# A neighbour search kept as marks, and softplus as one ScalarE function, in a graph-convolution and state-space kernel

## The chip, the cores and the metric

The kernel runs on one core of a Trainium2 chip. The metric is the time of one execution on the device in microseconds (us). Before the change the median of three runs is 13028.27 us (13025.54 to 13030.78). The engines are called PE (TensorE), DVE (VectorE), ACT (ScalarE), POOL (GpSimd) and SP (SyncE, which only issues DMAs here). Each works off its own queue of instructions.

## The reference

Two layers follow each other on x of shape (16, 96, 64, 64), all in fp32. Layer 0 is a graph convolution over windows of 8 x 8 pixels; for each of the 64 pixels of a window it finds the 9 nearest of the 64 by cosine distance, and takes the maximum over them:

```python
y = affine(conv1x1(x, fc1_w, fc1_b), fc1_s, fc1_t)
nodes = window_partition(y, 8).reshape(Bw, C, 64).transpose(0, 2, 1)
_, idx = jax.lax.top_k(-dist(nodes / norm), 9)
x_j = vmap(lambda n, i: n[i])(nodes, idx)
feat = concatenate([x_i, x_j - x_i], -1)            # x_i: the pixel itself
h = gelu((einsum('bnkc,oc->bnko', feat, ew) + eb) * es + et)
y = max(h, over the 9 neighbours)
x = affine(conv1x1(y, fc2_w, fc2_b), fc2_s, fc2_t) + x
```

Layer 1 has two Mamba blocks over the 4096 pixels in sequence (192 inner channels, 16 states), then a fusion with the pooled input, a batch normalisation and a residual:

```python
xc = silu(causal_conv4(h @ in_w)[..., :192]);  z = second half of h @ in_w
dt, Bm, Cm = split(xc @ xproj_w)
delta = softplus(dt @ dt_w + dt_b)
h_t = exp(delta * A) * h_(t-1) + delta * Bm * xc     # 16 states, 192 channels
y = (sum over the states of h_t * Cm + Dp * xc) * silu(z)
seq = seq + y @ out_w
```

## The kernel before

**Work and rows.** Layer 1 is cut into 256 items: 16 images, 2 blocks, 8 tiles of 512 pixels. The 192 channels and 16 states of an item are worked off in 8 rows, p = 0 to 7, of two states each, so that a row is a tile of 128 partitions by 3 x 512. There are 2048 rows, and the main loop (L871) makes one in each turn. A row is

- bt (`bcast`, L729): PE spreads B of the two states over the partitions, in the one PSUM buffer of its pool; it is issued at the head of the turn before,
- db (`times_b`, L734): DVE multiplies u = delta * xc by bt, at the end of the turn before, after that turn's scan,
- da (`chosen`, L708): ACT computes exp(delta * A), three instructions of 128 x 511, up to two rows ahead, into one of four buffers,
- hb (L911): DVE runs the recurrence as a scan over 1536 columns,
- hb times C (L943): POOL,
- y (`folded`, L745 and L747): PE adds the two states of each channel into PSUM, one turn later, at the end of the turn.

**Steps in the background.** All other work is written as generators, advanced by one step a turn between the scan and the fold: `prelude` of the next item but one (started in row 4, L888: projections pj with silu, xproj pd, softplus, delta and u), `norm`, `tail` (pow, the output product), `carry` (the state handed from tile to tile), and layer 0: `nearest` and `edges` of one image tile per 16 rows (the tiles 4 to 8 go faster, as do the first ones, ahead of the loop). So a cycle of 16 rows holds two items and one layer-0 tile, whose two halves (four windows each) have their gelu block in rows 2 and 3 and in rows 10 and 11. The order of each engine's queue is the order in which this program writes the instructions (`manual_schedule`, L807). A step that yields TABLE (gelu, silu) holds back the da of that turn, so that ACT changes its function table seldom; `preload_act_table_set` after the gelu block (L503) and after silu (L627) brings back the table of exp and ln.

**PSUM.** All background products share one pool, `pm` (L205), with two buffers under one tag, mm: a product can start once the product two before it in the program has been read out, mostly by ACT.

**Neighbours.** `nearest` computes the scores of a tile (sc, scs), then on DVE the 8 largest of each row (L396) and their positions (L397, `max_index`); the pixel itself is masked out of the scores beforehand and added later. The positions go to DRAM (L401) and come back to 64 partitions (L430, idb). `edges` makes one-hot matrices of them: for one pair of windows on POOL by a comparison (L441), for the other on ACT by |x - node| and relu(1 - x) (L443, L444). PE multiplies them with the transformed nodes (L468, L471); gelu follows (L476), and DVE takes the maximum over the neighbours (L413).

**Softplus.** In `prelude`, one step after pd and its copy dbl, in rows 0 and 8 of a cycle: the two dt products (L646 and L649, 128 x 512 and 128 x 256), from which ACT takes Abs and Relu out of PSUM (L653, L654), then Exp, + 1, Ln and - 1 over several rows (L656 to L662); POOL adds up (L672, L674, L676) so that small arguments keep their accuracy. Eight DMAs spread the result to delta over the partitions, POOL makes delta * xc (L681), and eight more spread it to u.

Of the kernel before, what the change touches and what calls it, by code (L numbers as in the profile page):

```python
# [21 lines left out]
def tile_conv_knn_mamba(ctx: ExitStack, tc: tile.TileContext, w: dict, out: bass.AP):  # L22
# [8 lines left out]
    nc = tc.nc  # L31
# [4 lines left out]
    NN = WS * WS  # L36
    K = 9
    KO = K - 1
# [28 lines left out]
    node = const.tile([NN, 1], F32, name="node")  # L67
    nc.gpsimd.iota(node, pattern=[[0, 1]], base=0, channel_multiplier=1, allow_small_or_imprecise_dtypes=True)
    minus_node = const.tile([NN, 1], F32, name="minus_node")
    nc.vector.tensor_scalar(minus_node, node, -1.0, None, ALU.mult)  # L70
# [237 lines left out]
    def half(h):  # L308
        return slice(h * CB, (h + 1) * CB)
# [21 lines left out]
    def nearest(b, q):  # L331
# [61 lines left out]
        idx = pr.tile([128, NP, KO], U16, tag="idx", name=f"idx_{nm}")  # L393
        for p in range(NP):
            m1 = pr.tile([128, KO], F32, tag="m1", name=f"m1_{nm}_{p}")
            nc.vector.max(m1, scs[:, p, :])  # L396
            opening.append(partial(nc.vector.max_index, idx[:, p, :], m1, scs[:, p, :]))  # L397
            yield SLOT

        idx_d = dram.tile([NP, 128, KO], U16, tag="idx_d", name=f"idxd_{nm}")  # L400
        nc.sync.dma_start(out=idx_d.rearrange("p i k -> i p k"), in_=idx)  # L401
        chosen_of[b, q] = idx_d
# [13 lines left out]
    def edges(b, q):  # L416
# [3 lines left out]
        idx_d = chosen_of.pop((b, q))  # L420
# [7 lines left out]
        for hf in range(2):  # L428
            idb = pr.tile([NN, NP, NN * KO], U16, tag="idb", name=f"idb_{nm}_{hf}", bufs=1)
            nc.sync.dma_start(  # L430
                out=idb.rearrange("j w n -> j (w n)"),
                in_=idx_d.rearrange("(s p) i k -> s (p i k)", s=2)[hf : hf + 1].to_broadcast([NN, NP * NN * KO]),
            )
            yield


            for p in (1, 0):
                ohj = ohs[p][0:NN].rearrange("j w i k -> j w (i k)")
                numbers = idb[:, 2 * p : 2 * p + 2, :]
                if p == 0:  # L440
                    nc.gpsimd.tensor_scalar(ohj, numbers, node, None, ALU.is_equal)  # L441
                else:
                    nc.scalar.activation(ohj, numbers, AF.Abs, bias=minus_node)  # L443
                    nc.scalar.activation(ohj, ohj, AF.Relu, bias=1.0, scale=-1.0)  # L444
                yield
# [147 lines left out]
    def prelude(n):  # L593
# [47 lines left out]


        e = pr.tile([128, Q + QH], F32, tag="e", name=f"e_{nm}", bufs=1)
        rl = pr.tile([128, Q + QH], F32, tag="rl", name=f"rl_{nm}", bufs=1)
        va = pm.tile([128, Q], F32, tag="mm", name=f"pdta_{nm}")
        nc.tensor.matmul(va, lhsT=dt_w[i][:, :128], rhs=dbl, start=True, stop=True)  # L646
        vb = pm.tile([128, QH], F32, tag="mm", name=f"pdtb_{nm}")
        for h in range(2):
            nc.tensor.matmul(  # L649
                vb[half(h)], lhsT=dt_w[i][:, 128:], rhs=dbl[:, bass.ts(h, QH)], start=True, stop=True  # L650
            )
# [5 lines left out]
        s1 = pr.tile([128, Q + QH], F32, tag="s1", name=f"s1_{nm}", bufs=1)  # L657
        nc.scalar.activation(s1, e, AF.Identity, bias=1.0)
        yield
        ln = pr.tile([128, Q + QH], F32, tag="ln", name=f"ln_{nm}", bufs=1)  # L660
        nc.scalar.activation(ln, s1, AF.Ln)
        nc.scalar.activation(s1, s1, AF.Identity, bias=neg1)  # L662
# [14 lines left out]
        yield  # L677
        delta = pr.tile([128, NB3, Q], F32, tag="delta", name=f"delta_{nm}")
# [192 lines left out]
    for m, (n, p) in enumerate(order):  # L871
# [17 lines left out]
        if p == 5 and k + 1 < NQ:  # L889
            going.append(carry(n + 1))  # L890
# [33 lines left out]
        if p == 0:  # L924
            step_on(preps)
# [88 lines left out]
```

## Time and profile before

The profiled execution took 13021.43 us, 7 us under the median of the runs; its span is 13019.7 us.

| engine | busy us | share of the span | largest groups, us |
|---|---|---|---|
| DVE | 11940.4 | 92% | scan L911 6863.5; db L734 3605.3; maximum L413 890.4 |
| POOL | 11686.0 | 90% | hb times C L943 7091.9; one-hot L441 731.0 |
| PE | 11254.7 | 86% | y L745 2273.8 and L747 1259.5; t L468 1012.8; pj L608 932.8 |
| ACT | 10407.8 | 80% | da L708 3937.7; gelu L476 1181.3; table loads 1050 of 1.283 us |

The mean granted clock of PE is 0.949. The first scan starts at 263 us and the last at 12814 us. Between, a cycle of 16 rows takes 97 us once the slow pace of layer 0 is reached.

How to read it: a group's line gives the line of the code, the engine, the operation, what it writes and reads, how many there are, their busy time and the mean of one, and then the idle time of the engine ahead of them with what ended it. A line of waits says who waited for whom, the total in us, how often and the longest. A line of the timeline gives start and length in us; "x4" are four merged instructions. A table of stages has, after the stage's length, the busy time of PE, of PE's weight loads, of DVE, ACT and POOL (with numbers of instructions), then PE's granted clock, the DMA share and GB/s. The names y and t, pf and so on are the tiles of the program without their numbers. The matmuls in fp32 stand in the trace as two instructions each.

### The profile page before, as it was taken

The numbers are of one execution on the slowest core, as the hardware profiler recorded it, in microseconds if no ns is written. First come the engines' busy times: TensorE is split into PE (matmuls) and PEld (weight loads), VectorE is DVE, ScalarE is ACT, GpSimd is POOL, SyncE is SP. The second block draws the span as 40 slices with busy tenths as digits, with TensorE's granted clock in tenths as the row PEclk, the third lists the DMA queues.
The fourth block names the chain that finished last, engine by engine and source line by source line (L and its number), as shares of the span: only waits on it lengthen the run. The fifth ranks groups of instructions, "written<-read, shape, count | busy, mean of one in ns | idle before, by whom it ended". The sixth has DMA issues, their size and how long they took to land.

```text
span 13019.7 us, 155850 instructions
## 1 busy us (share of the span) xinstructions
PE 11254.7 (86%) x46920; PEld 4359.3 (33%) x46920; DVE 11940.4 (92%) x8270; ACT 10407.8 (80%) x16186; POOL 11686.0 (90%) x8644
## 2 busy tenths in 40 slices
PE   5889889888989989888888888988888888889872
PEld 2333333333333333333333333333333333333320
DVE  2699999999999999999999999999999999999995
ACT  4778888888888888888888888888888888888763
POOL 3699999999999999999999999999999999999993
PEclk8899999999999999999999999999999999999986
DMA  1233333333333333333333333333333333333336
GB/s 38 66 85 95 91 91 93 94 92 89 98 89 90 96 92 90 93 94 89 95 95 87 98 92 90 94 92 93 90 95 92 90 95 93 92 89 97 89 87 261
DMA packets 1031198, 1226.82 MB, mean 94 GB/s; under 512 B 429440, under 2 KB 560910, under 8 KB 1024208
## 3 DMA queue, kind: packets, MB, share of 16 engines
q1 hardware_dynamic: 1026352, 1191.59, 35.2%
q10 hardware_dynamic: 4000, 25.28, 0.5%
q8 instruction: 370, 6.06, 0.2%
q14 instruction: 476, 3.90, 0.1%
HBM read 706.83 MB, written 85.72 MB: 61 GB/s over the span
## 4 chain that ended last, share of the span: by engine, by line
POOL 27%; PE 19%; DVE 18%; ACT 13%; issue 9%; DMA 7%; SPq 6%; POOLq 0%; DVEq 0%; ACTq 0%
POOL hb L943 16%; DVE hb L911 11%; DVE db L734 6%; ACT da L708 5%; PE y L745 3%; SPq L690 2%; SPq L692 2%; DMA ct<-cd 2%; POOL ln L674 2%; PE t L468 2%; PE y L747 1%; PE pj L608 1%; PE t L471 1%; POOL hn L591 1%; POOL ln L676 1%
## 5 line engine op out<-in xcount | busy, mean ns | idle before, releaser
L943 POOL TENSOR_TENSOR hb<-hb,ct 128x1536 f32<-128x1536 f32 x2048 | 7091.9, 3463 | 313.5 <-DVE hb L911 78.4
L911 DVE TENSOR_TENSOR_SCAN hb<-da,db 128x1536 f32<-128x1536 f32 x2048 | 6863.5, 3351 | 216.6 <-ACT da L708 39.4
L708 ACT ACTIVATE da<-delta,a 128x511 f32<-128x511 f32 x6144 | 3937.7, 713 | 28.7 <-DVE hb L911 24.1
L734 DVE TENSOR_TENSOR db<-u,bt 128x1536 f32<-128x1536 f32 x2048 | 3605.3, 1760 | 386.6 <-PE bt L729 266.3
L745 PE MATMUL y<-hb,fold 128*64 128x512 f32 x8192 | 2273.8, 634 | 230.4 <-POOL hb L943 219.7
L476 ACT ACTIVATE da<-t,eb,es 128x512 f32<-128x512 f32 x1536 | 1181.3, 777 | 775.3 <-PE t L468 534.7
L747 PE MATMUL y<-hb,fold 128*64 128x256 f32 x8192 | 1259.5, 386 | 0.0
L729 PE MATMUL bt<-bparts,bsel 128*128 128x512 bf16 x2048 | 828.4, 404 | 462.4 <-DVE db L734 459.3
L468 PE MATMUL t<-oh,vu 128*128 128x512 f32 x2048 | 1012.8, 616 | 27.2 <-ACT da L476 14.1
L747 PEld LDWEIGHTS y<-hb,fold 128*64 128x64 f32 x8192 | 604.2, 141 | 1247.6 <-issue 1247.6
L413 DVE TENSOR_REDUCE hq<-da 128x192 f32<-128x1536 f32 x512 | 890.4, 1739 | 105.4 <-ACT da L476 105.4
L608 PE MATMUL pj<-hn,conv_in 128*128 128x512 f32 x2048 | 932.8, 598 | 0.9 <-POOL hn L591 0.9
L745 PEld LDWEIGHTS y<-hb,fold 128*64 128x64 f32 x8192 | 495.0, 141 | 1278.5 <-issue 528.6
L441 POOL TENSOR_SCALAR oh<-idb,node 64x1024 f32<-64x1024 uint16 x256 | 731.0, 2855 | 117.2 <-DMA idb<-idxd 111.6
L452 PE MATMUL pv<-ewT,y 96*64 96x192 f32 x2048 | 477.6, 360 | 335.2 <-ACT rs L588 253.4
L942 POOL COPY state<-hb 128x3 f32<-128x3 f32 x1792 | 397.5, 222 | 392.3 <-DVE hb L911 359.0
L620 ACT ACTIVATE xc<-pj,conv_b 128x512 f32<-128x512 f32 (+1 forms) x512 | 297.2, 580 | 510.5 <-PE pj L613 397.8
L471 PE MATMUL t<-oh,vu 128*64 128x512 f32 x2048 | 560.4, 626 | 167.0 <-ACT da L476 162.3
L608 PEld LDWEIGHTS pj<-hn,conv_in 128*128 128x128 f32 x2048 | 396.4, 194 | 386.5 <-issue 375.7
L613 PE MATMUL pj<-hn,conv_in 128*64 128x256 f32 x4096 | 514.4, 394 | 0.0
L452 PEld LDWEIGHTS pv<-ewT,y 96*64 96x64 f32 x2048 | 253.0, 143 | 774.4 <-ACT rs L588 358.4
L468 PEld LDWEIGHTS t<-oh,vu 128*128 128x128 f32 x2048 | 373.5, 194 | 402.9 <-issue 290.3
(180 smaller groups left out, 17972.0 us busy)
## 6 DMA issues: line engine op xcount, KB each, us to landing
ct<-cd SPq DMA_DIRECT2D x4096, 128.0 KB
delta<-ln SPq DMA_DIRECT2D x1024, 128.0 KB
u<-s SPq DMA_DIRECT2D x1024, 128.0 KB
idb<-idxd SPq DMA_DIRECT2D x256, 256.0 KB
delta<-ln SPq DMA_DIRECT2D x1024, 64.0 KB
u<-s SPq DMA_DIRECT2D x1024, 64.0 KB
x<-in_x SPq DMA_DIRECT2D x128, 192.0 KB
rn<-r4d SPq DMA_DIRECT2D x128, 192.0 KB
```

The lines of the kernel that those rows point to most:

```text
L413: nc.vector.tensor_reduce(out(), g.rearrange("p s (i k) -> p s i k", k=KO), AX.X, ALU.max)
L441: nc.gpsimd.tensor_scalar(ohj, numbers, node, None, ALU.is_equal)
L468: nc.tensor.matmul(t, lhsT=vus[p][:, part, :128], rhs=ohw[part], start=True, stop=True)
L476: nc.scalar.activation(g, t, AF.Gelu, bias=e_b[:, j : j + 1], scale=e_s[:, j : j + 1])
L608: nc.tensor.matmul(ps, lhsT=wt[:, t, :128], rhs=hn[:, off : off + Q], start=(t == 0), stop=(t == taps - 1))
L708: nc.scalar.activation(da[:, c, 1:Q], delta[:, c, 1:], AF.Exp, scale=a_neg[i][:, c, p : p + 1])
L729: nc.tensor.matmul(bt, lhsT=bsel[:, p, :], rhs=made[n][2], start=True, stop=True)
L734: nc.vector.tensor_tensor(db, made[n][5], bt.unsqueeze(1).to_broadcast([128, NB3, Q]), ALU.mult)
L745: nc.tensor.matmul(y[half(h), 0], lhsT=fold, rhs=hb[:, h, :], start=False, stop=(p == NPR - 1))
L747: nc.tensor.matmul(y[half(h), 1, :QH], lhsT=fold, rhs=hb[:, 2, bass.ts(h, QH)], start=False, stop=(p == NPR - 1))
L911: nc.vector.tensor_tensor_scan(*(t.rearrange("p c q -> p (c q)") for t in (hb, das[at], db)), 0.0, ALU.mult, ALU.add)
L943: nc.gpsimd.tensor_tensor(hb, hb, ct.unsqueeze(1).to_broadcast([128, NB3, Q]), ALU.mult)
```

## The change

Two things are changed, and the steps of `prelude` are set anew.

*Neighbours as marks.* `max_index` becomes `match_replace`, which writes a mark (2^20) over the 8 largest scores in place. PE transposes the marked scores (eight products of 64 x 64, mp), and ACT makes 0 or 1 of them (mt, bf16). No positions go to DRAM. For each pair of windows PE then counts, with a triangular matrix, how many marked nodes stand before each node, plus 100 where the node itself is marked, less 100 + k for the k-th neighbour (two bf16 products into one tile of 128 x 512, `ranks`); the result is 0 exactly at the k-th marked node. ACT takes Abs of it out of PSUM (off, bf16) and relu(1 - x) in two halves (`onehot`). POOL's comparison and the two long ACT instructions go.

*Softplus as one function.* The two dt products and ACT's function Softplus straight out of PSUM take the place of the six ACT and three POOL steps. The step stands now eight steps after the start of the item's prelude, which is the turn in which the next item's prelude starts with its pj and silu: row 4 and row 12 of a cycle, the older prelude first. The built program has a table load ahead of softplus and another ahead of silu, 1307 loads in all (1050 before). delta is spread in the same row as before, u one row later (6 in place of 5). The extra step of `prelude` in row 0 goes. `carry` starts a row later and takes exp(a * delta) on ACT alone.

```diff
+    before = const.tile([128, 128], BF16, name="before")
+    sel0 = const.tile([128, 128], BF16, name="sel0")
+    krow = const.tile([128, Q], BF16, name="krow")
...
-            opening.append(partial(nc.vector.max_index, idx[:, p, :], m1, scs[:, p, :]))
+            opening.append(partial(nc.vector.match_replace, scs[:, p, :], m1, scs[:, p, :], MARK))
             yield SLOT
-        idx_d = dram.tile([NP, 128, KO], U16, tag="idx_d", name=f"idxd_{nm}")
-        nc.sync.dma_start(out=idx_d.rearrange("p i k -> i p k"), in_=idx)
-        chosen_of[b, q] = idx_d
+        ps = pm.tile([128, NP, NN], F32, tag="mm", name=f"mp_{nm}")
+        for h in range(2):
+            for p in range(NP):
+                nc.tensor.matmul(
+                    ps[half(h), p, :], lhsT=scs[half(h), p, :], rhs=ident[half(h), half(h)], start=True, stop=True
+                )
+        mt = pr.tile([128, NP, NN], BF16, tag="mt", name=f"mt_{nm}", bufs=3)
+        nc.scalar.activation(mt, ps, AF.Relu, bias=neg1, scale=2.0 / MARK)
+        chosen_of[b, q] = mt
...
-                if p == 0:
-                    nc.gpsimd.tensor_scalar(ohj, numbers, node, None, ALU.is_equal)
-                else:
-                    nc.scalar.activation(ohj, numbers, AF.Abs, bias=minus_node)
-                    nc.scalar.activation(ohj, ohj, AF.Relu, bias=1.0, scale=-1.0)
-                yield
+            def ranks(p):
+                ps = pm.tile([128, NN, KO], F32, tag="mm", name=f"rk_{nm}_{hf}_{p}")
+                nc.tensor.matmul(ps, lhsT=sel0, rhs=krow.rearrange("o (i k) -> o i k", k=KO), start=True, stop=False)
+                marks = mt[:, 2 * hf + p, :].unsqueeze(2).to_broadcast([128, NN, KO])
+                nc.tensor.matmul(ps, lhsT=before, rhs=marks, start=False, stop=True)
+                off = pr.tile([128, NN, KO], BF16, tag="off", name=f"off_{nm}_{hf}_{p}")
+                nc.scalar.activation(off, ps, AF.Abs)
+                return off
+            def onehot(p, off):
+                for h in range(2):
+                    nc.scalar.activation(ohs[p][0:NN, h], off[half(h)], AF.Relu, bias=1.0, scale=-1.0)
+            off = ranks(1)
+            yield
+            onehot(1, off)
+            off = ranks(0)
+            yield
+            onehot(0, off)
+            yield
...
         nc.sync.dma_start(out=c_d, in_=dbl[NS : 2 * NS, :])
+        yield
...
+        yield
+        yield
+        yield
         va = pm.tile([128, Q], F32, tag="mm", name=f"pdta_{nm}")
         nc.tensor.matmul(va, lhsT=dt_w[i][:, :128], rhs=dbl, start=True, stop=True)
...
-        for v, cols in ((va, slice(0, Q)), (vb, slice(Q, Q + QH))):
-            nc.scalar.activation(e[:, cols], v, AF.Abs)
-            nc.scalar.activation(rl[:, cols], v, AF.Relu)
-        yield
-        nc.scalar.activation(e, e, AF.Exp, scale=-1.0)
-        nc.scalar.activation(s1, e, AF.Identity, bias=1.0)
-        yield
-        nc.scalar.activation(ln, s1, AF.Ln)
-        nc.scalar.activation(s1, s1, AF.Identity, bias=neg1)
...
-        nc.gpsimd.tensor_tensor(e, e, s1, ALU.subtract)
-        yield
-        nc.gpsimd.tensor_tensor(ln, ln, e, ALU.add)
-        yield
-        nc.gpsimd.tensor_tensor(ln, ln, rl, ALU.add)
-        yield
+        sp = pr.tile([128, Q + QH], F32, tag="sp", name=f"sp_{nm}", bufs=1)
+        nc.scalar.activation(sp[:, :Q], va, AF.Softplus)
+        nc.scalar.activation(sp[:, Q:], vb, AF.Softplus)
         delta = pr.tile([128, NB3, Q], F32, tag="delta", name=f"delta_{nm}")
-        doubled(delta, ln)
+        doubled(delta, sp)
+        yield
         u = pr.tile([128, NB3, Q], F32, tag="u", name=f"u_{nm}")
-        nc.gpsimd.tensor_tensor(s1, ln, xc, ALU.mult)
+        up = pr.tile([128, Q + QH], F32, tag="up", name=f"up_{nm}", bufs=1)
+        nc.gpsimd.tensor_tensor(up, sp, xc, ALU.mult)
         made[n] = (xc, z, bp, c_d, delta, u)
         yield
-        doubled(u, s1)
+        doubled(u, up)
...
-        d0 = made[n][4][:, :, 0:1].to_broadcast([128, NB3, NPR])
-        nc.gpsimd.tensor_tensor(first, a_neg[i], d0, ALU.mult)
-        yield
-        nc.scalar.activation(first, first, AF.Exp)
+        delta = made[n][4]
+        for c in range(NB3):
+            nc.scalar.activation(first[:, c], a_neg[i][:, c], AF.Exp, scale=delta[:, c, 0:1])
...
-        if p == 5 and k + 1 < NQ:
+        if p == 6 and k + 1 < NQ:
             going.append(carry(n + 1))
...
-        if p == 0:
-            step_on(preps)
```

More of the change, by code (lines that the diff above doesn't have):

```diff
@@ L66, in tile_conv_knn_mamba @@
     nc.vector.tensor_scalar(cmat, ident[:C, :C], -1.0 / C, None, ALU.add)
[L67 to L70, printed above, removed]
+    FAR = 100.0
+    MARK = 2.0**20
+    before = const.tile([128, 128], BF16, name="before")
+    sel0 = const.tile([128, 128], BF16, name="sel0")
+    krow = const.tile([128, Q], BF16, name="krow")
+    nc.vector.memset(sel0, 0.0)
+    nc.vector.memset(sel0[0:1], 1.0)
+    nc.vector.memset(krow, 0.0)
+    for k in range(KO):
+        nc.vector.memset(krow[0:1].rearrange("o (i k) -> o i k", k=KO)[:, :, k], -FAR - k)
+    with tc.tile_pool(name="order", bufs=1) as sp:
+        lower = sp.tile([128, 128], F32, name="lower")
+        nc.gpsimd.memset(lower, 1.0)
+        nc.gpsimd.affine_select(
+            out=lower, in_=lower, compare_op=ALU.is_gt, fill=0.0, base=0, pattern=[[1, 128]], channel_multiplier=-1
+        )
+        nc.vector.memset(lower[:NN, NN:], 0.0)
+        nc.vector.scalar_tensor_tensor(before, ident, FAR, lower, ALU.mult, ALU.add)
     neg1 = const.tile([128, 1], F32, name="neg1")
@@ L392, in nearest @@
         yield
-        idx = pr.tile([128, NP, KO], U16, tag="idx", name=f"idx_{nm}")
         for p in range(NP):
@@ L396, in nearest @@
             nc.vector.max(m1, scs[:, p, :])
-            opening.append(partial(nc.vector.max_index, idx[:, p, :], m1, scs[:, p, :]))
+            opening.append(partial(nc.vector.match_replace, scs[:, p, :], m1, scs[:, p, :], MARK))
             yield SLOT
-        idx_d = dram.tile([NP, 128, KO], U16, tag="idx_d", name=f"idxd_{nm}")
-        nc.sync.dma_start(out=idx_d.rearrange("p i k -> i p k"), in_=idx)
-        chosen_of[b, q] = idx_d
+        ps = pm.tile([128, NP, NN], F32, tag="mm", name=f"mp_{nm}")
[3 more added lines that the diff above has]
+                    ps[half(h), p, :], lhsT=scs[half(h), p, :], rhs=ident[half(h), half(h)], start=True, stop=True
+                )
+        mt = pr.tile([128, NP, NN], BF16, tag="mt", name=f"mt_{nm}", bufs=3)
+        nc.scalar.activation(mt, ps, AF.Relu, bias=neg1, scale=2.0 / MARK)
+        chosen_of[b, q] = mt
     def taken():
@@ L419, in edges @@
         y = nodes_of.pop((b, q))
-        idx_d = chosen_of.pop((b, q))
+        mt = chosen_of.pop((b, q))
         maxima = []
@@ L428, in edges @@
         for hf in range(2):
[L429 to L433, printed above, removed]
-            yield
-            for p in (1, 0):
-                ohj = ohs[p][0:NN].rearrange("j w i k -> j w (i k)")
-                numbers = idb[:, 2 * p : 2 * p + 2, :]
-                if p == 0:
-                    nc.gpsimd.tensor_scalar(ohj, numbers, node, None, ALU.is_equal)
-                else:
-                    nc.scalar.activation(ohj, numbers, AF.Abs, bias=minus_node)
-                    nc.scalar.activation(ohj, ohj, AF.Relu, bias=1.0, scale=-1.0)
-                yield
+            def ranks(p):
[10 more added lines that the diff above has]
+            off = ranks(1)
+            yield
+            onehot(1, off)
[3 more added lines that the diff above has]
+            yield
             vus = []
@@ L640, in prelude @@
         nc.sync.dma_start(out=c_d, in_=dbl[NS : 2 * NS, :])
[L643 to L651, printed above, removed]
-        for v, cols in ((va, slice(0, Q)), (vb, slice(Q, Q + QH))):
-            nc.scalar.activation(e[:, cols], v, AF.Abs)
-            nc.scalar.activation(rl[:, cols], v, AF.Relu)
-        yield
-        nc.scalar.activation(e, e, AF.Exp, scale=-1.0)
-        s1 = pr.tile([128, Q + QH], F32, tag="s1", name=f"s1_{nm}", bufs=1)
-        nc.scalar.activation(s1, e, AF.Identity, bias=1.0)
-        yield
-        ln = pr.tile([128, Q + QH], F32, tag="ln", name=f"ln_{nm}", bufs=1)
-        nc.scalar.activation(ln, s1, AF.Ln)
-        nc.scalar.activation(s1, s1, AF.Identity, bias=neg1)
+        yield
         b3 = pr.tile([128, 3, QS], BF16, tag="b3", name=f"b3_{nm}")
@@ L671, in prelude @@
             nc.sync.dma_start(out=bp[r : r + NS], in_=b3[:, part])
-        nc.gpsimd.tensor_tensor(e, e, s1, ALU.subtract)
         yield
-        nc.gpsimd.tensor_tensor(ln, ln, e, ALU.add)
         yield
-        nc.gpsimd.tensor_tensor(ln, ln, rl, ALU.add)
         yield
+        va = pm.tile([128, Q], F32, tag="mm", name=f"pdta_{nm}")
+        nc.tensor.matmul(va, lhsT=dt_w[i][:, :128], rhs=dbl, start=True, stop=True)
+        vb = pm.tile([128, QH], F32, tag="mm", name=f"pdtb_{nm}")
+        for h in range(2):
+            nc.tensor.matmul(
+                vb[half(h)], lhsT=dt_w[i][:, 128:], rhs=dbl[:, bass.ts(h, QH)], start=True, stop=True
+            )
+        sp = pr.tile([128, Q + QH], F32, tag="sp", name=f"sp_{nm}", bufs=1)
+        nc.scalar.activation(sp[:, :Q], va, AF.Softplus)
+        nc.scalar.activation(sp[:, Q:], vb, AF.Softplus)
         delta = pr.tile([128, NB3, Q], F32, tag="delta", name=f"delta_{nm}")
-        doubled(delta, ln)
+        doubled(delta, sp)
+        yield
         u = pr.tile([128, NB3, Q], F32, tag="u", name=f"u_{nm}")
-        nc.gpsimd.tensor_tensor(s1, ln, xc, ALU.mult)
+        up = pr.tile([128, Q + QH], F32, tag="up", name=f"up_{nm}", bufs=1)
+        nc.gpsimd.tensor_tensor(up, sp, xc, ALU.mult)
         made[n] = (xc, z, bp, c_d, delta, u)
         yield
-        doubled(u, s1)
+        doubled(u, up)
     def doubled(t, src):
```

## The prediction

> **What bounds the kernel now.** I read the page's busy times first, then the slices, the table of stages, the waits of VectorE and TensorE, and last the timeline of one repeating stretch.
>
> ```profile
> PE 11254.7 (86%) x46920; PEld 4359.3 (33%) x46920; DVE 11940.4 (92%) x8270; ACT 10407.8 (80%) x16186; POOL 11686.0 (90%) x8644
> ...
> DVE  2699999999999999999999999999999999999995
> POOL 3699999999999999999999999999999999999993
> ```
>
> ```profile
> 1000.00:12000.00 11000.00, 9840.15 (x41455) 3813.66 (x41453) 10478.91 (x7256) 9113.20 (x14253) 10321.83 (x7615) 0.97 0.36 92
> ```
>
> Between 1000 and 12000 us DVE is busy 10479 of 11000 us and idle 521. A row's scan (3.35) and product with B (1.76) alone make 5.1 us. So the bound is DVE, with POOL (94%) and PE (89%) close behind.
>
> ```profile
> DVE db L734 <- PE bt L729: 266.3, 171, 14.2
> ...
> PE bt L729 <- DVE db L734: 459.3, 289, 5.2
> ```
>
> Each waits for the other over bt, the broadcast of B: one PSUM buffer, written by PE, read by DVE at the head of the next row. PE can be one bt ahead and no more, and a bt stands in PE's queue behind all that the row before put there. So what counts is whether PE reaches the next bt while DVE scans. The stretch that decides is this one, row 12 to 16 of a 16-row cycle:
>
> ```profile
> 6332.66 0.55 ACT L496 ACTIVATE sa<-tb,eb,es 128x256 f32<-128x256 f32 x1
> 6333.23 1.28 ACT L503 ACT_TABLE_LOAD   x1
> ...
> 6333.98 3.60 PE L608 MATMUL pj<-hn,conv_in 128*128 128x512 f32 x8
> 6334.53 3.78 ACT L708 ACTIVATE da<-delta,a 128x511 f32<-128x511 f32 x6
> ...
> 6338.33 1.28 ACT L620 ACT_TABLE_LOAD   x1
> ...
> 6338.95 0.39 PE L729 MATMUL bt<-bparts,bsel 128*128 128x512 bf16 x1
> ...
> 6339.63 0.69 ACT L620 ACTIVATE xc<-pj,conv_b 128x512 f32<-128x512 f32 x1
> ...
> 6342.18 1.76 DVE L734 TENSOR_TENSOR db<-u,bt 128x1536 f32<-128x1536 f32 x1
> ...
> 6350.44 0.39 PE L729 MATMUL bt<-bparts,bsel 128*128 128x512 bf16 x1
> ...
> 6353.93 1.76 DVE L734 TENSOR_TENSOR db<-u,bt 128x1536 f32<-128x1536 f32 x1
> ```
>
> See that PE starts the convolution pj at 6333.98, while ACT, done with gelu, still has a table load, six decay exponentials and another load before it (6333.23 to 6339.6). PE works ahead of ACT here. The bt behind pj ends at 6339.34, 2.84 us before DVE takes it (6342.18); the bt two rows on ends at 6350.83, 3.10 us before its use (6353.93). That is all the slack.
>
> **The change, part by part.**
>
> POOL loses four large groups: 731.0 (one-hot compare), 464.4, 463.6 and 464.3 (softplus sums), and 51.6 (L717): 2175 us, to 73% of the span. DVE waited for POOL hardly at all: POOL first 8.8 us, POOL hn 3.5, and 29.2 for the PE fold that frees hb. So this buys at most some 40 us of DVE time; what covers it is DVE's own work, and I take 0. POOL's remaining work gets earlier, and DVE is next late for nothing of POOL's.
>
> DVE swaps max_index (81 + 218 ns, 512 times) for match_replace. Nearest rows: FIND_INDEX8 218, MAX8 202, so 0 by the first; reading and rewriting 64 columns bounds it at -40 to +60 us. Taken 0.
>
> DMA: 384 issues go (idx, its two broadcasts). DVE idles nowhere for them in the steady stage; PE and ACT did not wait for their landing there either (the idb waits, 111.6 and 63.7, are 13 long ones, of the beginning). For the beginning I take -20, between -60 and 0.
>
> ACT loses 2006 us: Abs and Relu of softplus (152.8 + 100.4 + 151.6 + 103.7), Exp, Identity, Ln, Identity (218.7 + 215.9 + 214.7 + 239.7), one-hot (290.4 + 270.6), first (46.3). It gains softplus 253 (as L653; with a pointer operand, as L620's 687, some 25 more), 512 Abs over ranks at 0.60 = 307, 1024 half one-hots at 0.53 (half of L444's 1057) = 541, mt 128 x 0.37 = 47, carry 672 x 0.2 = 134 and 257 table loads at 1.28 = 330: 1612. So 394 us less in sum. Since ACT is at 80%, the sum matters little; where the work stands matters.
>
> PE gains mp (1024 small ones; as L389, 170.1 us for as many) and ranks, 1024 bf16 matmuls that pass about every 0.21 us (from bt's start to the start of the next matmul): 215. Their broadcast operand is in no row; the fp32 products of L608 pass every 0.45, which is the upper bound (1 us a half more). I take bt's, being bf16 as they are.
>
> u is doubled one row later (row 6, not 5). Behind the eight delta DMAs (0.6 us each, released by softplus) and ct, u's eight end some 14 us after softplus and land 3 us later; the db that needs it comes 19 us after. Covered; if SP were late by more than 2 us it would become a wait. carry starts a row later but is a step shorter.
>
> **The step that decides: softplus moved in front of pj.** Before, the two dt products (L646, L649) stood in rows 0 and 8, far from pj. Now they stand in rows 4 and 12 directly ahead of pj in PE's queue, and softplus on ACT is behind the two da sets of that row. The mm ring has two buffers: dt product a takes one, b the other, pj needs a's back. In the changed program pj's first matmul waits for the first softplus. Behind pj in PE's queue stand the folds, the next bt, ranks, the rest of the projection, folds, bt.
>
> Second half of a cycle: ACT reaches the place of today's silu load at 6338.33, plus 0.28 for mt (L391's 0.37 less overlap); load 1.30; softplus 0.60 (L653): 6340.5. So pj starts at 6340.55 in place of 6333.98: 6.57 late. PE has mp and the dt products meanwhile (3.0 us) and then nothing for 3.3 us. From pj's start to the end of the first bt is 5.36: 6345.9, against 6342.18: DVE waits 3.7. To the end of the bt at row 16 it was 16.85; add two ranks (0.85) and a new wait of 1.3: the pow product needs the buffer of the second ranks, whose Abs stands on ACT behind silu 0.38, load 1.30, da 1.94 and one-hots 1.05, itself 0.60 = 5.3, while PE has 4.0 (fold 1.4, bt 0.35, ranks 0.45, pd 1.85). So 6359.55 against 6353.93: DVE is 5.6 late in all.
>
> First half (row 4), from its own timeline: silu's load stood at 6290.32, softplus ends at 6292.2, pj starts at 6292.25 in place of 6285.74; first bt 6297.6 against its use at 6295.08, 2.5 late; last bt 6292.25 + 16.85 + 0.85 + 1.3 = 6311.25 against 6305.77, 5.5 late. PE idles 4.6 us ahead of pj.
>
> Those gaps cost clock:
>
> ```profile
> 6315.20:6318.70 3.50, 0.03 (x2) 0.05 (x1) 3.47 (x4) 3.47 (x7) 3.42 (x5) 1.00 0.44 108
> 6318.70:6322.10 3.40, 3.38 (x7) 1.55 (x8) 3.40 (x4) 3.38 (x7) 3.40 (x2) 0.52 0.08 24
> ```
>
> After 3.5 us without matmuls PE ran the next 3.4 us at 0.52 of its clock, that is 1.7 us of work lost. For the first half's 4.6 us I take 1.7, for the second's 3.3 us half of it, 0.85 (between 0 and 1.7 each).
>
> Sum of a cycle: 5.5 + 1.7 + 5.6 + 0.85 = 13.65 us. DVE, being the bound, never makes it up; in rows 1 to 3 and 9 to 11 PE catches up with DVE, so the lateness doesn't add from one half to the next. Rows 3 and 11 keep today's bt waits, since PE's order there is unchanged (0, between -1.7 and +1 a cycle). Image tiles 9 to 127 run at this pace, one per 16 rows: 119 x 13.65 = 1624. The five faster-paced tiles before them: between 0 and 10 x 6.8 = 68, taken 35. The twelve last items have no gelu ahead of softplus; ACT is ahead there: 0.
>
> 13021 (the profiled execution; its span is 13020) + 1624 + 35 - 20 = 14660; the median of the runs shown is 7 above that execution, so 14670.
>
> [...]
>
> **The rivals.**
>
> *Only the first bt is late.* PE makes good the rest before the second, and the clock holds: 2.5 + 3.7 = 6.2 a cycle, 119 x 6.2 = 738, 13780 in all. For it: PE has 11% idle in the steady stage. Against it: PE's timeline has no gap from pj to row 16.
>
> *Faster.* If softplus came within 2.84 us of pj's present start (the slack above; 3.13 in the first half), no bt would be late, and DVE's waits for bt, fold and first (169 + 28 + 9 us of the steady stage) could go: 13028 - 206 = 12820. That needs the gelu block to end 3.7 us sooner. Against it: gelu is paced by PE's t products, whose waits (534.7 + 207.8 us) ACT already has, and these start at a bt that DVE releases.
>
> *ACT becomes the bound behind softplus.* The da set of row 7 is computed within 0.1 us of need in my count. If ACT is 1 us later there, each half adds 1: 238, 14910.
>
> *Softplus shares silu's set.* Then 257 loads, 330 us of ACT, vanish, and pj's wait shrinks by nothing, for the load ahead of softplus stays. The changed program lists both loads, so I give it no chance of its own.
>
> **How the numbers follow.** Both bts late, with or without the clock's share (14350 to 14800): 0.65. First bt only: 0.18. ACT late besides: 0.12. Faster: 0.05, of which 0.01 goes to no change; a measurement of this kernel tells 0.2% (26 us) from nothing. The range is 13750 to 14950: from the first rival's time, widened by the 40 us of DVE's swap, to the third's with it. Slower 0.95.
>
> **What would show it.** Of the changed kernel: DVE db waiting for PE bt rises from 266 to some 1600 to 1900 us; TensorE's pj (L633) waits for ACT sp, 3 to 5 us, 256 times; DVE's busy time stays at 11940 within 60; POOL falls near 9500, ACT near 10000; the granted clock of the steady stage falls below 0.97. I am wrong if pj starts without that wait, or if DVE's waits for bt stay below 500 us: then softplus comes sooner than I count, and the faster case is near.

## The result and the profile after

The changed kernel takes 14685.76 us (median of six runs, 14682.56 to 14696.89) against 13031.35 us for the kernel before in the same comparison (six runs, 13025.54 to 13036.69). The ratio is 1.1271, 95% interval 1.1257 to 1.1286: 12.7% slower. The prediction was 14670 us with a range of 13750 to 14950.

The busy times of the profiled execution (span 14680.8 us), and the table of the steady stage with DVE's busy time third behind the length (9147.32) and the granted clock of PE (0.93):

```profile
PE 11935.0 (81%) x49992; PEld 4701.3 (32%) x49992; DVE 11938.8 (81%) x8282; ACT 10251.4 (70%) x16507; POOL 9619.5 (66%) x7397
```

```profile
1000.00:12000.00 11000.00, 9170.86 (x38574) 3616.85 (x38576) 9147.32 (x6327) 7836.93 (x12696) 7417.14 (x5679) 0.93 0.29 76
```

DVE works as long as before (11940.4), but in the steady stage it now idles 1853 of 11000 us instead of 521. No engine is full any more: the engines wait for each other in turn. Who waits for whom (total us, how often, longest):

```profile
DVE db L748 <- PE bt L743: 1970.3, 543, 10.6
...
PE pj L633 <- ACT sp L689: 989.9, 253, 6.1
...
PE bt L743 <- DVE db L748: 589.2, 298, 5.2
...
PE pow L786 <- ACT off L456: 365.3, 237, 1.8
```

Two of these did not exist before: pj behind softplus (3.9 us each) and pow behind the Abs of the ranks (1.54 us each). The first line was 266.3 us. The group of the convolution products, pj, shows the wait as its idle time and one thing more: its mean rose from 598 to 902 ns.

```profile
L633 PE MATMUL pj<-hn,conv_in 128*128 128x512 f32 x2048 | 1504.7, 902 | 990.7 <-ACT sp L689 989.9
```

The place itself, rows 12 to 16 of one cycle, in the timeline:

```profile
7341.75 0.96 PE L416 MATMUL mp<-ident,scs 64*64 64x64 f32 x16
...
7342.20 1.94 ACT L723 ACTIVATE da<-delta,a 128x511 f32<-128x511 f32 x3
...
7342.64 1.12 PE L682 MATMUL pdta<-dbl,dt_w 128*128 128x512 f32 x2
...
7344.41 1.93 ACT L723 ACTIVATE da<-delta,a 128x511 f32<-128x511 f32 x3
...
7344.56 0.65 PE L685 MATMUL pdtb<-dbl,dt_w 128*64 128x256 f32 x4 [0.80 <-ACT mt L420]
...
7346.36 1.28 ACT L689 ACT_TABLE_LOAD   x1
...
7347.65 0.60 ACT L689 ACTIVATE sp<-pdta 128x512 f32<-128x512 f32 x1
...
7348.30 6.39 PE L633 MATMUL pj<-hn,conv_in 128*128 128x512 f32 x8 [3.09 <-ACT sp L689]
...
7356.07 0.39 PE L743 MATMUL bt<-bparts,bsel 128*128 128x512 bf16 x1
...
7356.50 1.76 DVE L748 TENSOR_TENSOR db<-u,bt 128x1536 f32<-128x1536 f32 x1 [6.35 <-PE bt L743]
...
7365.26 0.57 ACT L456 ACTIVATE off<-rk 128x512 bf16<-128x512 f32 x1
...
7365.89 1.10 PE L786 MATMUL pow<-z,out_w 128*96 128x512 f32 x2 [1.59 <-ACT off L456]
```

The large dt product is done at 7343.8, but ACT reaches softplus only behind two sets of da and a table load, and pj, which needs that product's buffer, starts 0.05 us after the first softplus ends. Then its eight matmuls take 6.39 us where they took 3.60. The table of stages tells why: the last figures of each line are clock, DMA share and GB/s.

```profile
7345.21:7348.30 3.09, 0.01 (x1) 0.00 (x0) 3.09 (x3) 3.06 (x5) 0.29 (x1) 0.78 0.00 0
7348.30:7351.70 3.40, 3.40 (x4) 1.51 (x5) 1.84 (x1) 1.51 (x2) 3.02 (x3) 0.50 0.52 115
7351.70:7354.70 3.00, 3.00 (x7) 1.03 (x7) 0.00 (x0) 0.00 (x0) 2.34 (x1) 0.66 0.65 140
```

After the 3.09 us gap PE runs 3.4 us at half its clock and part of the next 3 us.

Read as DVE's time from scan to scan, mean of 118 steady cycles (rows 61 to 1949). A row's time runs from the scan of the row before to its own scan; rows 6 and 14 use the first bt behind pj, rows 8 and 0 the bt two rows on. The kernels beside the first two are the experiments below:

| row of the cycle | before | after | marks only | softplus only | no load | PE busy | ranks early |
|---|---|---|---|---|---|---|---|
| 6 | 5.50 | 9.78 | 5.49 | 9.62 | 7.69 | 8.45 | 9.88 |
| 8 | 5.64 | 8.37 | 5.63 | 6.06 | 8.37 | 8.37 | 6.37 |
| 14 | 5.55 | 11.50 | 5.56 | 11.31 | 8.56 | 9.20 | 11.16 |
| 0 | 5.54 | 7.78 | 6.27 | 5.54 | 7.78 | 7.78 | 6.22 |
| 1 | 5.49 | 5.49 | 8.45 | 5.61 | 5.49 | 5.49 | 5.49 |
| 3 and 4 | 13.88 | 12.79 | 14.70 | 12.88 | 12.79 | 12.79 | 12.79 |
| cycle of 16 | 97.25 | 111.34 | 103.55 | 106.74 | 106.25 | 107.67 | 108.76 |

118 x 14.09 = 1663 us; ahead of row 61 the changed kernel is 12 us faster, behind row 1949 11 us slower; together the 1661 us between the two spans.

### The profile page after: what moved, and what is told of

Its sections match the earlier page's. It is cut to its first block, busy times and chain, and to the rows that moved or that the text cites. A ratio compares the mean times of both kernels' runs of the same rounds, so it can differ in the third digit from the quotient of the medians.

```text
span 14680.8 us, 159777 instructions
## 1 busy us (share of the span) xinstructions
PE 11935.0 (81%) x49992; PEld 4701.3 (32%) x49992; DVE 11938.8 (81%) x8282; ACT 10251.4 (70%) x16507; POOL 9619.5 (66%) x7397
## 4 chain that ended last, share of the span: by engine, by line
PE 45%; ACT 31%; DVE 11%; SPq 5%; DMA 3%; issue 3%; POOL 1%; ACTq 0%; DVEq 0%; POOLq 0%
ACT da L723 13%; PE pj L633 8%; DVE hb L925 7%; PE y L759 7%; PE t L493 5%; PE t L496 4%; DVE db L748 4%; PE y L761 3%; PE pj L638 2%; ACT L689 2%; ACT L528 2%; PE bt L743 2%; SPq L707 2%; SPq L705 2%; PE pow L786 2%
## 5 line engine op out<-in xcount | busy, mean ns | idle before, releaser
L925 DVE TENSOR_TENSOR_SCAN hb<-da,db 128x1536 f32<-128x1536 f32 x2048 | 6863.6, 3351 | 188.9 <-ACT da L723 53.1
L633 PE MATMUL pj<-hn,conv_in 128*128 128x512 f32 x2048 | 1504.7, 902 | 990.7 <-ACT sp L689 989.9
L633 PEld LDWEIGHTS pj<-hn,conv_in 128*128 128x128 f32 x2048 | 578.2, 297 | 1805.8 <-ACT sp L689 1105.0
L761 PEld LDWEIGHTS y<-hb,fold 128*64 128x64 f32 x8192 | 633.2, 141 | 1213.7 <-issue 1176.8
L759 PEld LDWEIGHTS y<-hb,fold 128*64 128x64 f32 x8192 | 515.4, 140 | 1001.4 <-issue 566.1
L696 POOL TENSOR_TENSOR up<-sp,xc 128x768 f32<-128x768 f32 x256 | 462.0, 1805 | 431.1 <-ACT sp L690 431.0
L462 ACT ACTIVATE oh<-off 64x512 f32<-64x512 bf16 x1024 | 638.4, 623 | 7.0
L786 PE MATMUL pow<-z,out_w 128*96 128x512 f32 x512 | 283.5, 636 | 366.1 <-ACT off L456 365.3
L456 ACT ACTIVATE off<-rk 128x512 bf16<-128x512 f32 x512 | 299.4, 585 | 362.9 <-PE rk L454 362.9
```

Of the source, the lines that this page charges most:

```text
L633: nc.tensor.matmul(ps, lhsT=wt[:, t, :128], rhs=hn[:, off : off + Q], start=(t == 0), stop=(t == taps - 1))
L759: nc.tensor.matmul(y[half(h), 0], lhsT=fold, rhs=hb[:, h, :], start=False, stop=(p == NPR - 1))
L761: nc.tensor.matmul(y[half(h), 1, :QH], lhsT=fold, rhs=hb[:, 2, bass.ts(h, QH)], start=False, stop=(p == NPR - 1))
L925: nc.vector.tensor_tensor_scan(*(t.rearrange("p c q -> p (c q)") for t in (hb, das[at], db)), 0.0, ALU.mult, ALU.add)
```

## The experiments

The ring theory is the prediction's: pj is held by softplus through the two-buffer PSUM ring. Its rivals: the neighbours' products and waits, the table loads by themselves, or the longer queue of PE make the loss.

### Each half of the change alone

The first kernel is the one before with the neighbours' hunks only (marks, mp, ranks, one-hots); the old softplus stays.

```diff
-            opening.append(partial(nc.vector.max_index, idx[:, p, :], m1, scs[:, p, :]))
+            opening.append(partial(nc.vector.match_replace, scs[:, p, :], m1, scs[:, p, :], MARK))
...
+            off = ranks(1)
+            yield
+            onehot(1, off)
+            off = ranks(0)
```

> The kernel before with the neighbours half of the change alone: marks, ranks and one-hots by ScalarE; softplus stays as it was, in its old places. Ring theory (pj, held by its PSUM buffer until softplus has run, makes the loss): pj starts where it did before, so the first bt of a half is not late; to the second bt come two ranks (0.85 us) and the wait of the pow product (1.3), 2.15 us against 3.1 us of slack, so nearly all is covered: 12900 to 13150 us, and VectorE's wait for bt stays near the 266 us of before. Rival (the added TensorE products and the new wait of pow make the loss): 2 x 5 us a cycle stay, 119 x 10 = 1190 us, 14000 to 14500.

Measured: 13748.31 us, ratio 1.0554 (1.0539 to 1.0568). Neither expectation: pj was not held and rows 6 and 14 stayed as before (the table), but the kernel lost 722 us elsewhere, 3.0 of its 6.3 us a cycle in row 1. Its timeline around rows 0 and 1:

```profile
6885.45 1.10 PE L797 MATMUL pow<-z,out_w 128*96 128x512 f32 x2 [1.59 <-ACT off L456]
...
6893.88 1.10 PE L540 MATMUL pf<-x,ident 96*96 96x512 f32 x2 [1.46 <-ACT rl L679]
...
6898.09 0.39 PE L754 MATMUL bt<-bparts,bsel 128*128 128x512 bf16 x1
```

The wait of pow, 1.6 us, was foreseen. The second was not: in this kernel the old dt products stand one turn behind it, and the second half of the one-hots now stands on ACT in front of their Abs and Relu; so the next product, pf, waits for a PSUM buffer as pj does in the changed kernel. Both halves of the change use the same ring.

The second kernel has the softplus half only, at its new place. For softplus stands the sigmoid, so its output is not the reference's.

```diff
+        nc.scalar.activation(sp[:, :Q], va, AF.Sigmoid)
+        nc.scalar.activation(sp[:, Q:], vb, AF.Sigmoid)
```

> The kernel before with the softplus half of the change alone, at its new place directly ahead of pj; neighbours as positions, as before. In place of softplus stands the sigmoid, which has a table set of its own as softplus has and is as many ScalarE instructions of the same shape; so the output is not the reference's. Ring theory: pj waits for the function as in the changed kernel, 253 long waits; what falls away is ranks and the wait of pow, 2.15 us a half, and the products for the marks (some 1 us ahead of pj). 14.1 - 4.3 = 9.8 us a cycle x 119 = 1170: 14200, between 13900 and 14600. Rival (the neighbours half makes the loss): 13000 to 13300.

Measured: 14171.03 us, ratio 1.0875 (1.0859 to 1.0892), within 30 us of the ring theory's figure. Its waits:

```profile
DVE db L723 <- PE bt L718: 1504.0, 578, 13.6
...
PE pj L608 <- ACT sp L664: 1163.7, 253, 6.1
...
ACT L664 <- PE pdta L657: 78.0, 11, 8.2
```

The last line is that of the table load ahead of the sigmoid; the load ahead of softplus in the changed kernel waits 75.4 us for the same product. pj waits the same 253 times, rows 6 and 14 are as late as with the whole change, and rows 8 and 0 hardly at all: 0.42 and 0.00 us instead of 2.73 and 2.24. Those two rows need both halves: with the marks alone row 8 loses nothing and row 0 0.73 us, and only behind a late pj does the wait of pow come on top. The two halves cost 722 + 1145 = 1867 us alone and 1654 us together (the difference of the medians). Together they lose 3.8 us a cycle more in rows 8 and 0 than apart, but with softplus moved the collision of row 1 is gone (3.0 us), and rows 3, 4, 10 and 12 lose 2.7 us less.

### The place of softplus

The changed kernel with the dt products and softplus in the turns in which the old dt products stood (that is five turns earlier; the expectation says three):

```diff
         nc.sync.dma_start(out=c_d, in_=dbl[NS : 2 * NS, :])
+        va = pm.tile([128, Q], F32, tag="mm", name=f"pdta_{nm}")
...
+        nc.scalar.activation(sp[:, :Q], va, AF.Softplus)
+        nc.scalar.activation(sp[:, Q:], vb, AF.Softplus)
+        nc.scalar.preload_act_table_set("natural_log_exp_and_others")
         yield
```

> The changed kernel with the dt products and the one-function softplus moved back to right behind the projection's DMAs (three turns earlier, where the old dt products stood), far from pj; the exp set is loaded once more behind it, so it has more table loads than the changed kernel (two a prelude added instead of one). Ring theory: pj starts unheld again, waits of pj for ScalarE's softplus fall from 990 us to under 50, VectorE's waits for bt from 1970 to under 500: 13050 to 13150, between 12900 and 13350. Rival (the loss is the table loads and ScalarE's time itself): no better than the changed kernel, 14700 to 15000.

Measured: 13636.67 us, ratio 1.0467 (1.0453 to 1.0482). 1049 us came back although its program has one table load more a prelude, so their number by itself is not the cause; but it misses the expected 13050 to 13150 by 487. The mistake is the one of the first experiment:

```profile
DVE db L749 <- PE bt L744: 883.8, 453, 10.1
...
PE pow L787 <- ACT off L456: 320.7, 237, 1.6
...
PE pf L540 <- ACT sp L674: 285.7, 119, 2.4
```

pj no longer waits for softplus, but the same ring now stops pf, 119 times 2.4 us: row 1 takes 10.09 us. Softplus was not put out of the way, only in front of another product.

Next, softplus one turn earlier than in the change, straight behind the gelu block, with the set of exp loaded behind softplus instead of behind gelu:

```diff
-            nc.scalar.preload_act_table_set("natural_log_exp_and_others")
+            if not follows:
+                nc.scalar.preload_act_table_set("natural_log_exp_and_others")
...
-        yield
         va = pm.tile([128, Q], F32, tag="mm", name=f"pdta_{nm}")
...
         nc.scalar.activation(sp[:, Q:], vb, AF.Softplus)
+        nc.scalar.preload_act_table_set("natural_log_exp_and_others")
```

> The changed kernel with the dt products and softplus one turn earlier, straight behind the gelu block and ahead of the decay exponentials of the next turns; the exp set that gelu would load behind itself is loaded once, behind softplus, so the number of table loads is that of the changed kernel. Ring theory: softplus ends some 4 to 5 us earlier and pj is held by 1 to 2 us at most, inside the slack of 2.8 to 3.1 us; ranks and the wait of pow can still push the second bt by up to 1 us a half: 12900 to 13350. Rival (the dt products in front of pj cost by themselves, wherever ScalarE has softplus, as 3 us of products and marks more in TensorE's queue): 13700 to 14700.

Measured: 13331.09 us, ratio 1.0232 (1.0218 to 1.0246), inside the ring theory's range, at its upper end. The dt products stand in front of pj on PE here too, one turn earlier, with that turn's folds, the next bt and mp between; PE has the same work ahead of pj, but ACT now has softplus ahead of the da sets. pj's mean is back at 598 ns, and the waits are

```profile
DVE db L750 <- PE bt L745: 490.0, 288, 10.7
...
PE pow L788 <- ACT off L457: 364.7, 237, 1.6
...
PE pj L635 <- ACT sp L690: 5.3, 4, 1.3
```

So 1355 us of the loss went with pj's wait for ACT's late softplus and the clock behind it; the products' own length on PE, which is unchanged, is no part of them. Row 6 takes 5.49 and row 14 5.56 us again.

### What the wait is made of

The changed kernel with the exponential for softplus (no table load ahead of it, 16250 instructions on ACT instead of 16507; output not the reference's):

```diff
-        nc.scalar.activation(sp[:, :Q], va, AF.Softplus)
-        nc.scalar.activation(sp[:, Q:], vb, AF.Softplus)
+        nc.scalar.activation(sp[:, :Q], va, AF.Exp)
+        nc.scalar.activation(sp[:, Q:], vb, AF.Exp)
```

> The changed kernel with the exponential in the place of softplus: the same two instructions at the same place, but the table set is the one that the decay exponentials ahead of them have loaded, so the load ahead of softplus falls away (the output is then not the reference's). Ring theory: pj is still held, by 1.3 us less a half: 2 x 1.3 x 119 = 310 less, 14370; if the second half's gap of 3.3 us shrinks so far that the clock is not lowered there, 1.7 x 119 = 200 less again, 14170. So 14150 to 14400. Rival (the added table loads are the loss, by a cost beyond their own 1.28 us): back to the neighbours' share alone, 13600 to 13800.

Measured: 14076.92 us, ratio 1.0805 (1.0788 to 1.0821): 609 us less, some 75 more than the largest gain in the ring theory's range. pj starts 1.43 us earlier in both halves (median against the scan of rows 4 and 12). The rest is clock: pj's length falls from 6.08 to 5.43 us in the first half and from 5.94 to 4.51 in the second (means of the same 118 cycles; 3.60 before). 2 x 1.43 + 0.65 + 1.43 = 4.9 us of the 5.09 us that a cycle gains.

The changed kernel with the small dt products repeated, so that PE works while it waits:

```diff
-        for h in range(2):
-            nc.tensor.matmul(
-                vb[half(h)], lhsT=dt_w[i][:, 128:], rhs=dbl[:, bass.ts(h, QH)], start=True, stop=True
-            )
+        for _ in range(5):
+            for h in range(2):
+                nc.tensor.matmul(
+                    vb[half(h)], lhsT=dt_w[i][:, 128:], rhs=dbl[:, bass.ts(h, QH)], start=True, stop=True
+                )
```

> The changed kernel with the two small dt products (vb) computed five times over, ahead of pj: the same result into the same buffer, and TensorE has some 2.6 us of work in the gap in which it waited for softplus. pj is held just as long. If the lowered clock behind the gap costs 1.7 us in each half (as the two traces suggest): 2 x 1.7 x 119 = 405 less, 14280, and pj's first products take 0.45 us again instead of 0.9. If the clock is a symptom without a price (TensorE catches up, or the wait for softplus alone sets the bt): 14650 to 14720.

Measured: 14257.81 us, ratio 1.0943 (1.0926 to 1.0959), 428 us less for 4096 more matmul instructions. PE's timeline of a second half:

```profile
7131.07 2.38 PE L686 MATMUL pdtb<-dbl,dt_w 128*64 128x256 f32 x20 [0.80 <-ACT mt L420]
7134.81 3.70 PE L633 MATMUL pj<-hn,conv_in 128*128 128x512 f32 x8 [1.37 <-ACT sp L690]
```

pj starts as late as in the changed kernel (7.01 and 9.95 us behind the scan of rows 4 and 12 in both, medians), but runs at full clock behind a gap of 1.37 us. In the first half the gap is still 3.2 us, and pj still takes 4.76 us in the mean. So the lowered clock is a cost of its own: 428 us of it were won back here.

### The second bt

The changed kernel, both rank products and their Abs one turn earlier:

```diff
-            off = ranks(1)
+            offs = [ranks(1), ranks(0)]
             yield
-            onehot(1, off)
-            off = ranks(0)
+            onehot(1, offs[0])
             yield
-            onehot(0, off)
+            onehot(0, offs[1])
```

> The changed kernel itself, with only the ranks moved: both rank products of a half and their Abs are issued together, one turn earlier. pj is held by softplus as before. If the wait of pow for the second Abs is a cost that comes on top of pj's (the prediction had 1.3 us a half for it; the traces show 1.6): 2 x 1.5 x 119 = 360 less, 14330, between 14250 and 14430. If pj's lateness alone sets the second bt too: 14650 to 14720.

Measured: 14376.81 us, ratio 1.1032 (1.1015 to 1.1049): 309 us less, and the wait of pow is gone from the list while pj's is unchanged:

```profile
DVE db L747 <- PE bt L742: 1549.8, 505, 10.6
...
PE pj L632 <- ACT sp L688: 989.5, 253, 6.1
```

Rows 8 and 0 fall by 2.00 and 1.56 us, row 7 rises by 0.76. The wait of pow comes on top of pj's.

The same edit on the kernel of the neighbours' half alone, with the second rank product behind the folds of its row:

```diff
+            behind_fold.append(second)
             yield
             onehot(1, offs[0])
...
+        while behind_fold:
+            behind_fold.pop(0)()
```

> The kernel of the neighbours half alone (13748), with the second rank product and its Abs issued one turn earlier, behind the folds of that row; softplus in its old steps. In that kernel two new waits stand ahead of the second bt: pow for the second Abs (347 us, 237 times) and the next PSUM product for Abs and Relu of the dt products, which stand on ScalarE behind the second one-hots (173 us, 119 times). If both add up to the loss: taking the first away gives 350 to 400 less, 13350 to 13400, and the other stays. If the loss is the added TensorE work itself: 13650 to 13750. If the one wait hides the other: 13500 to 13650.

Measured: 13425.68 us, ratio 1.0302 (1.0286 to 1.0317), 323 us less; the waits of pf stay as they were:

```profile
DVE db L767 <- PE bt L762: 629.1, 367, 10.2
...
PE pf L548 <- ACT rl L687: 173.5, 119, 1.5
```

The two new waits add up, with 27 us of the expected 350 missing. Of the 387 us that remain against the kernel before in the same comparison (3.6 us a cycle), row 1 has 2.0 us. The rest, in rows 3, 4, 10 and 12, is again mostly DVE waiting for bt (in row 12 1.07 us a cycle against 0.45 before); what holds PE there I did not trace.

### Towards a version without the loss

The kernel at 13331 us with the same early ranks:

```diff
-            off = ranks(1)
+            offs = [ranks(1), ranks(0)]
```

> The kernel with softplus straight behind the gelu block (13331), and both rank products of a half with their Abs issued together, one turn earlier, so that the pow product no longer waits for the second Abs behind the one-hots (365 us of such waits there, 237 times, 1.6 us each). If that wait is what holds the second bt of each half (rows 0 and 8, where VectorE idles 2.2 and 1.5 us against 0.3 and 0.4 before): 119 x (1.9 + 1.1) = 360 less, 12970, between 12930 and 13080, about the kernel before. Rival (the two ranks' own time on TensorE and ScalarE holds it, wherever they stand): 13280 to 13350.

Measured: 13099.89 us, ratio 1.0051 (1.0037 to 1.0064): 231 us less, 20 us over the expected interval. Against before, rows 3 and 4 gain 1.10 us, rows 0, 13 and 15 lose 0.51, 1.03 and 0.30. Three more edits went after rows 13 and 0. The first puts both dt products of turn 3 behind the row's folds and the next bt, and the second rank product behind the folds:

```diff
+        if p == 3:
+            if preps and m + 2 < len(order):
+                early.append(bcast(*order[m + 2]))
+            held |= step_on(preps)
```

> The kernel with softplus straight behind the gelu block and early ranks (13100), with two orders mended. First, the dt products of turns 3 and 11 are issued behind that row's folds and behind the next bt instead of ahead of them; softplus keeps its place on ScalarE. Second, the second rank product and its Abs stand behind the row's folds instead of in front of the rest of the projection. There VectorE's rows 12, 13 and 0 are still 0.1, 1.0 and 0.5 us longer than before and row 15 0.3, rows 3 and 4 together 1.0 shorter. If the places on TensorE's queue are the reason: rows 13 and 0 go back, 119 x 1.5 = 180 less, 12920, between 12870 and 13030: faster than before by 0 to 1.2%. Rival (ScalarE, now later with softplus by the wait for its products, holds pj instead): 13100 to 13300.

Measured: 13311.23 us, ratio 1.0210 (1.0196 to 1.0223). The rival held in its direction, 11 us beyond its range, though not by pj, which waits 17.8 us for softplus in all: softplus and all behind it on ACT came later, and the scans now wait for their da, the first of these lines:

```profile
DVE hb L935 <- ACT da L733: 294.6, 261, 4.8
DVE db L758 <- PE bt L753: 284.0, 227, 10.6
```

In the last two only the small dt product goes behind the bt, with the second rank product late or early:

```diff
         nc.scalar.activation(sp[:, :Q], va, AF.Softplus)
+        yield
         vb = pm.tile([128, QH], F32, tag="mm", name=f"pdtb_{nm}")
```

> The kernel with softplus straight behind the gelu block, and the second rank product behind that row's folds (as in the try at 13311); of the dt products only the small one (vb, 0.65 us) is issued behind the next bt, the large one stays in front of the folds, so that softplus of the large one starts as early as at 13100. Theory (TensorE is full from the gelu products to row 0; the bt of rows 13 and 0 are late by what stands in front of them): row 13 0.65 us and row 0 0.5 us shorter than at 13100, 119 x 1.1 = 130 less, 12970, between 12900 and 13050. Rival (ScalarE's decay exponentials, 0.4 us later behind the second softplus, hold the scans of rows 13 and 14): 13100 to 13250.

> As the kernel at 13100 (softplus straight behind the gelu block, both rank products of a half together one turn early), with the small dt product (vb, 0.65 us) issued behind the next bt, the large one in front of the folds as there. Theory: the bt of row 13 comes 0.65 us earlier, and nothing else moves: 119 x 0.65 = 77 less, 13020, between 12980 and 13060, level with the kernel before. Rival (ScalarE's decay exponentials, 0.4 us later behind the second softplus, hold the scans of rows 13 and 14): 13100 to 13250.

Measured: 13221.75 us, ratio 1.0145 (1.0129 to 1.0160), and 13274.64 us, ratio 1.0190 (1.0176 to 1.0204). The rival held in both, the second 25 us beyond its range. DVE waits for ACT's da 175.7 and 144.2 us there, against 49.2 us in the kernel at 13100 (the last of these three views):

```profile
DVE hb L936 <- ACT da L734: 175.7, 306, 4.9
```

```profile
DVE hb L927 <- ACT da L725: 144.2, 263, 4.8
```

```profile
DVE hb L926 <- ACT da L724: 49.2, 105, 4.8
```

Row 13 stays at 9.50 us: its wait for bt falls from 0.95 to 0.22 us a cycle, but a wait of 0.67 us for da takes its place. Row 14 goes from 5.60 to 6.02. In the second kernel the waits for da are 95 of the 175 us that it lost; rows 7 and 8, each 0.31 us longer, were not taken apart. No version here beats the kernel before.

## Why the prediction was right

The forecast missed the median by 16 us and the direction and the mechanism were right: pj, held through the ring of two buffers by a softplus that stands behind two da sets and a load, and two late bt in each half. The sizes of its terms, in us a cycle:

| term | predicted | measured | by |
|---|---|---|---|
| pj later, first and second half | 6.51, 6.57 | 6.39, 6.26 | pj against the scan of rows 4 and 12 |
| clock in pj, both halves | 1.7 + 0.85 | 2.48 + 2.34 | pj's mean length 6.08 and 5.94 against 3.60 |
| first bt, with the clock | 4.2, 4.55 | 4.28, 5.95 | rows 6 and 14 |
| second bt on top | 3.0, 1.9 | 2.73, 2.24 | rows 8 and 0 |
| rows 3 and 4 | 0 | -1.09 | the table |
| cycle | 13.65 | 14.09 | |

**The clock was undersized by half.** The prediction took 1.7 us for the gap ahead of the first half and half of that for the second's. Both cost more. The row that it went by showed a half clock for 3.4 us; behind these gaps it lasts for 4.8 and 4.5 us of pj in the mean, and the 3.09 us gap (the median) lowers it as surely as the 4.92 us one: 117 and 118 of 118 times (pj longer than 5 us). The "one half" between 0 and 1.7 had no row behind it.

**What made up for it.** "Rows 3 and 11 keep today's bt waits" was wrong on the good side: the bt wait of row 4 fell from 1.02 to 0.10 us a cycle, and rows 3 and 4 gain 1.09 us. The two rows take 12.79 to 12.90 us wherever the one-function softplus stands, and 14.70 with the marks alone, so the gain comes with the softplus half. The waits show its way: PE's pv, which stands ahead of that bt, waits for ACT's rs in the kernel before, and hardly in the changed one:

```profile
PE pv L452 <- ACT rs L588: 253.4, 121, 3.1
```

```profile
PE pv L477 <- ACT rs L613: 47.3, 120, 3.0
```

With the marks alone that wait is 254.7 us, with softplus alone 50.4, so by these waits the old softplus steps held that bt through rs (their Ln and - 1 stand ahead of it on ACT, 1.8 us long); which of them did, was not tried.

And without the clock the first half's first bt is 1.9 us late (7.01 + 3.60 + 1.76, from pj's start to the end of bt, against its use 10.43 us behind the scan of row 4), not 2.5. These errors of opposite sign bring the sum within 0.5 us of the measured cycle, and outside the 118 cycles the prediction had some 29 us (a 119th cycle, and 35 - 20) where -12 + 11 were measured; so the closeness of the total is partly luck.

**The terms that were tested and held.** The wait of pow, 1.3 us a half, gives 2 x 1.3 x 119 = 309 us, and taking it away from the changed kernel gave 309. That the two agree so well is chance: the wait itself was 1.54 us (the two one-hots ahead of the second Abs took 1.25 us, not 1.05), and the edit that took it away made row 7 longer by 0.76. The load ahead of softplus cost 1.43 us a half. The load's own 1.28 us is nearly all of it; the kernel without that load shows at most 0.15 us besides.

**A sum that would have failed alone.** By the sum of the neighbours' half (2.15 us against 3.1 us of slack at the second bt) it would cost next to nothing by itself. In rows 8 and 0 it did cost little, 0.73 us a cycle, but by itself that half cost 722 us, most of it in other rows: 323 us went with the wait of pow, and pf waited 173 us behind the one-hots that stand in front of the old Abs and Relu. The prediction didn't need it, the first two expectations did.

**What was to be seen.** DVE's waits for bt came to 1970 us (70 above the 1600 to 1900 forecast), pj's for softplus 253 times 3.9 us (3 to 5), DVE's busy time 11938.8 (11940), POOL's 9619.5 (9500), the steady clock 0.93 (below 0.97). ACT's work fell by 156 us, not 394: the half one-hots took 0.62 us each (0.53 taken, 95 us) and the three carry instructions 0.29 each (0.2, 60 us); the longer one-hots are in pow's wait, above. That POOL's 2066 us bought nothing, as forecast, no run shows by itself; DVE's waits for POOL were 12 us before. The rival of one late bt a half is refuted by rows 8 and 0, the faster one by pj's waits. The rival of ACT behind softplus does not show in the changed kernel (DVE waits 53.1 us for da there), though it does in the last three experiments.

One slip: the text before and the prediction put the old dt products in rows 0 and 8; counted by the turns of the loop they are issued in turns 7 and 15. No term used it.

## What to carry to other kernels

When a step moves, ask of every queue it touches what stands in front of it there: softplus as one function was cheap (0.60 and 0.38 us an item), but behind two decay sets and a load on ACT it held a PSUM buffer that PE's next product needed, and the same instructions directly behind the gelu block cost 1355 us less. Price an idle gap of PE twice, once as the wait and once as the clock behind it; the second can be told from the first by giving PE throwaway work in the gap (428 us of clock here). Two halves of a change that share a ring don't add: here they cost 722 and 1145 us alone, and 1654 together.

## What the runs showed of the hardware that was not expected

PE's granted clock fell to 0.50 for 3.4 us behind a gap of 3.09 us, which followed 0.65 us of work and a gap of 0.80 us; pj took 5.94 us in the mean instead of 3.60. Behind gaps of 1.36 us (medians here; second half, PE busy) pj kept full speed 117 of 118 times; behind 1.66 us (second half, no load) it was slow 58 times of 118, and behind 3.2 us (first half, PE busy) 71 times of 118, so in these runs the length of the gap alone doesn't decide it. In the traces of the changed kernel and of the kernel before, the records of the granted clock have two values, 1.00 and 0.50, and all begin a multiple of 3.413 us apart. In the changed kernel 374 stretches of that length at full clock were filled by PE's matmuls to less than 40%, and every one of them was followed by half clock; of the 3236 fuller ones 15 were. In the kernel before it was 170 of 170, and 89 of 3230. So here a gap of 3.09 us, shorter than a stretch, was enough, with little work around it.
